# Attention scores from split operands: twelve-bit key and query halves on 128 rows, one full-array pass for each key tile, fetched per unit from DRAM

## The chip, the core and the metric

The kernel runs on one core of one Trainium2 chip. A core has five engines that run their own instruction streams and meet through semaphores: TensorE (PE, matrix products into PSUM; its weight loads have a row of their own in the profile, PEld), VectorE (DVE), ScalarE (ACT), GpSimd (POOL) and SyncE (SP, which here only issues DMA transfers). ACT and POOL can issue DMA transfers too. The metric is the device time of one execution in microseconds (us); lower is better.

## What is computed

Four images of 256 channels and 64 x 64 pixels go through a self-attention layer over the 4,096 pixels, and then through a clustering block with an MLP. The part that matters here is the attention's score matrix:

```python
C = 256
CQK = C // 8                       # 32
xf = x.reshape(B, Cc, N)           # N = 4096
q = jnp.einsum('oc,bcn->bno', wq, xf) + bq
k = jnp.einsum('oc,bcn->bon', wk, xf) + bk[None, :, None]
attn = jax.nn.softmax(jnp.einsum('bnd,bdm->bnm', q, k), axis=-1)
v = jnp.einsum('oc,bcn->bon', wv, xf) + bv[None, :, None]
out = jnp.einsum('bcn,bmn->bcm', v, attn).reshape(B, Cc, H, W)
x = gamma[0] * out + x
...
y = x + ls1 * cluster(group_norm(x))
y = y + ls2 * mlp(group_norm(y))
z = relu(batch_norm(y * dw_w)); z = relu(batch_norm(conv1x1(z, pw_w)))
```

A score is a product over only 32 values of the head, while every other large product is over 128 channels at a time. All inputs and outputs are float32.

## The kernel before

**Units.** The score matrix of an image is made transposed, keys on the 128 partitions and queries along the free axis. A *unit* is 512 keys (four tiles of 128) against one block of 512 queries; there are 8 x 8 = 64 units in an image, numbered u = 8 * nb + g with nb the query block and g the key group. `score(u)` (line 364) makes the four 128 x 512 tiles of a unit, copies them from PSUM to SBUF on ACT (lines 382 and 387) and takes the running maximum on DVE (lines 386 and 389). `exps(u)` subtracts the maximum (DVE, line 465), takes the exponential (ACT, line 468) and adds up the sums (POOL, line 473). `weigh(u, ...)` multiplies with the values (TensorE, line 478: eight matmuls a unit, "av" in the profile).

**Operands of the scores.** `k_half(i)` projects half of the keys (line 292) so that the key tile r of a group lies on partitions 32r to 32r + 31, and ACT evacuates it into the SBUF tile `k` (line 299). `q_four(i)` projects four query blocks, one on each 32 partitions (line 334), and ACT evacuates them (line 342). `q_block(nb)` (line 349) copies one block to all four groups of 32 partitions with four DMA transfers from SBUF to SBUF, issued on ACT's queue (on POOL's at the start, on SP's between images). Thus the four matmuls of a unit each use 32 rows of the array, on different rows.

**Order.** The order on every engine is written by hand. For each image:

- *Alone* (first image only): k_half(0), q_four(0), two q_blocks, then the units 0 to 7 with a pair of value projections (`v_pair`, line 315) after each; k_half(1) stands before unit 3.
- *Weighting*: 64 units; in unit u stand `exps(u + 1)`, `score(u + 10)` and the eight av matmuls of u. Each query block also has two row transfers through DRAM (`everywhere`, lines 84 and 85, SP's queue) that spread the maximum and the sum. `q_four(1)` stands at the end of unit 17.
- *Cluster* and *MLP*: while these run, the projections of the next image (`v_half`, `k_half`, `q_four`) are put in as filler at hand-chosen places by `fill(n)`. k_half(0) and q_four(0) stand after `similar(1)` and before `affine(0)` (line 819) and `largest(0)`, a chain on DVE that TensorE's product at line 904 waits for; k_half(1) stands before the second normalization. Eight scores of the next image, units 0 to 7, stand in the cluster's end and the MLP.

**Buffers.** SBUF tiles come from pools by tag. The tag "acc" has one buffer and is shared by the exponentials' sums, the odd normalized blocks, `g` (line 972) and the odd hidden tiles of the MLP; "w2" and "q4" also have one buffer each, "q" has two. A new tile under a tag waits until all readers of the last one are done. PSUM tag "m" has two buffers.

Of the kernel before, what the change touches and what calls it, by code (L numbers as in the profile page):

```python
# [7 lines left out]

F32 = mybir.dt.float32
AF = mybir.ActivationFunctionType  # L10
ALU = mybir.AluOpType
AX = mybir.AxisListType

P = 128
B, C, H, W = 4, 256, 64, 64
N = H * W
KC = C // P
NB = 512
NBLK = N // NB
XT = 1024  # L20
D = 32
# [7 lines left out]
RG, GRP = 4, N // NB  # L29
# [16 lines left out]
def attention_then_cluster_block(  # L46
# [17 lines left out]
    nc = tc.nc  # L64
# [3 lines left out]
    big = ctx.enter_context(tc.tile_pool(name="big", bufs=1))  # L68
# [4 lines left out]
    work = ctx.enter_context(tc.tile_pool(name="work", bufs=2))  # L73
# [202 lines left out]
    def attention(b, xs):  # L276
# [2 lines left out]
        own = {}  # L279
        stats = small.tile([P, 2 * NBLK, 6], F32, tag="stats", name=f"st1_{b}")  # L280
        cells = small.tile([P, KC, NBLK, 4], F32, tag="cells", name=f"cells_{b}")
        qs, slots, mxs, accs, tops, rdens, ts = {}, {}, {}, {}, {}, {}, {}

        def k_half(i):

            if i == 0:
                own["k"] = big.tile([P, GRP, P], F32, tag="k", name=f"k_{b}")
            ps = ps_m.tile([P, 2, 2, P], F32, tag="m", name=f"kp_{b}_{i}")
            for t in range(2):
                for k in range(KC):  # L290
                    for r in range(RG):
                        nc.tensor.matmul(
                            ps[r * D : (r + 1) * D, t],
                            wqk_s[:, k, 1],
                            xs[2 * i + t][:, k].rearrange("p (g r n) -> p r g n", g=2, r=RG)[:, r],
                            start=(k == 0),
                            stop=(k == KC - 1),
                        )
            nc.scalar.activation(
                own["k"][:, 4 * i : 4 * i + 4, :].rearrange("p (t g) n -> p t g n", t=2),  # L300
                ps,
                AF.Identity,
                bias=bqk_s[:, 1:2],
            )

        vps = {}

# [18 lines left out]
            v_half(2 * i)  # L326
            v_half(2 * i + 1)

        def q_four(i):

            ps = ps_m.tile([P, NB], F32, tag="m", name=f"qp_{b}_{i}")
            for k in range(KC):
                for r in range(RG):
                    nc.tensor.matmul(  # L334
                        ps[r * D : (r + 1) * D],
                        wqk_s[:, k, 0],
                        block(xs, k, 4 * i + r),
                        start=(k == 0),
                        stop=(k == KC - 1),
                    )  # L340
            own["q"] = work.tile([P, NB], F32, tag="q4", bufs=1, name=f"q4_{b}_{i}")
            nc.scalar.activation(own["q"], ps, AF.Identity, bias=bqk_s[:, 0:1])

        def q_block(nb, dma=nc.scalar):

            qs[nb] = work.tile([P, NB], F32, tag="q", name=f"q_{b}_{nb}")
            r = nb % 4
            for g in range(RG):
                dma.dma_start(
                    out=qs[nb][g * D : (g + 1) * D], in_=own["q"][r * D : (r + 1) * D]  # L350
                )

        def score(u, hooks=None, later=None):

            nb, g = divmod(u, GRP)
            q_s, k_s = qs[nb], own["k"]
            pool, tag = (swap, "w1") if u % (SLOTS + 1) == SLOTS else (spool, "s")
            s = slots[u] = pool.tile([P, RG, NB], F32, tag=tag, name=f"s_{b}_{u}")
            halves = [
                ps_s.tile([P, 2, NB], F32, tag="s", name=f"sc_{b}_{u}_{h}") for h in range(2)  # L360
            ]
            for r in range(RG):
                rows = slice(r * D, (r + 1) * D)
                nc.tensor.matmul(  # L364
                    halves[r // 2][:, r % 2, :], k_s[rows, g, :], q_s[rows, :], start=True, stop=True
                )
            if g == 0:
                tops[nb] = work.tile([P, 2, NB], F32, tag="top", bufs=1, name=f"top_{b}_{nb}")
# [163 lines left out]
        def alone():  # L532

            k_half(0)
            q_four(0)
            q_block(0, nc.gpsimd)
            q_block(1, nc.gpsimd)
            for i in range(4):
                v_pair(i)
            for u in range(GRP):  # L540
                if u == RG - 1:
                    k_half(1)
                hooks, maxima = [], []
                score(u, hooks, maxima)
                for f in hooks + maxima:
                    f()
                v_pair(u + 4)
            fold(0)
            for i in range(GRP + 4, GRP + 6):
                v_pair(i)  # L550
            half["dg"] = across(0)
            v_pair(GRP + 6)
            spread(0, half["dg"])
            v_pair(GRP + 7)
            exps(0)
            score(GRP)
# [26 lines left out]
        def weighting(ahead, fill, early):  # L583
# [3 lines left out]
            for u in range(units):  # L587
# [48 lines left out]
                        xs[t][:, c], xs[t][:, c], AF.Identity, bias=gbv[:, c : c + 1]  # L636
                    )
                if u == 2 * GRP + 1:
                    q_four(1)
                if g == 3 and nb + 2 < NBLK:  # L640
                    q_block(nb + 2)
                if g == GRP - 1 and more:
# [39 lines left out]

        parts = Parts()
        parts.xs, parts.alone, parts.weighting = xs, alone, weighting
        parts.score, parts.fold, parts.q_block = score, fold, q_block
        parts.maximum, parts.first, parts.exps = maximum, first, exps
        parts.projections = [lambda i=i: v_half(i) for i in range(N // P)]
        parts.projections[26:26] = [lambda: k_half(1)]
# [6 lines left out]
    def cluster(b, ys, stats, cells, rest, fill, gelu, nxt, maxima):  # L695
# [338 lines left out]
            fill(6)  # L1034
            return stats2

        nxt.q_block(0, nc.sync)
        fill(4)
        copies = []
        nxt.score(0, copies, maxima)  # L1040
# [120 lines left out]
    def mlp(b, ys, stats2, fill, nxt, blocks, turned, maxima):  # L1161
# [310 lines left out]
        for nb in range(blocks):  # L1472
            end = nb == blocks - 1
            for j in range(4):
# [12 lines left out]
                if j == 0:  # L1487
# [11 lines left out]
                    elif nxt:  # L1499

                        nc.sync.dma_start(
                            out=a21_s, in_=w2.rearrange("(k p) m -> p k m", p=P)[:, :h_n, P:]
                        )
                        nxt.q_block(1, nc.sync)
                elif j == 1:
                    assert not drips and not hooks
                    if nb:
# [155 lines left out]
```

## Time and profile before

| | before |
|---|---|
| median of 3 runs | 3339.82 us (3339.4 to 3340.23) |
| span of the profiled execution | 3338.8 us |
| mean granted TensorE clock | 0.997 of full speed |
| 256 units' scores: records on TensorE, busy time | 2,048, 299.8 us |
| av: records, busy time | 4,096, 1819.2 us |
| DMA traffic | 70.97 MB, 21 GB/s on average |

In the profile, "busy" of a group is the time in which at least one of its instructions ran; "mean" is one instruction from its start to its end, which is longer than the distance to the next, since matmuls overlap. "32*128" behind a matmul says how many rows and columns of the array it uses, "128x512" is partitions by elements, "idle before" is what the engine waited, and for whom. The chain of waits follows the last instruction back to whatever released it.

What the transfers cost, by the list of DMA issues (KB of each, and us from issue to landing):

```profile
out<-xn SPq DMA_DIRECT2D x62, 256.0 KB, 2.1
...
mr<-row_mx SPq DMA_DIRECT2D x28, 256.0 KB, 3.1
...
q<-q ACTq DMA_DIRECT2D x96, 64.0 KB, 2.0
```

And by the instructions of one line (lengths in ns, min/median/max, of the issue itself on its queue):

```profile
L349 ACTq DMA_DIRECT2D q<-q x96: 513/602/640, 92.7 to 2873.3; - x96
L349 SPq DMA_DIRECT2D q<-q x24: 513/582/1099, 617.8 to 2477.7; - x24
```
```profile
L1250 SPq DMA_DIRECT2D out<-xn x62: 332/332/1299, 694.5 to 3335.5; - x62
```

### The profile page before, as it was taken

Reading aid. Unit: us, or ns where it says so; the run is one execution under the profiler, and the core shown is the slowest. Engines: PE = TensorE matmul, PEld = TensorE weight load, DVE = VectorE, ACT = ScalarE, POOL = GpSimd, SP = SyncE. Lnnn points to the kernel's source line nnn. Section 1 sums busy time; section 2 is a strip of 40 time slices with the busy share of each in tenths; the row PEclk is TensorE's granted clock in tenths of the full one; section 3 lists DMA queues with packets and bytes.
Section 4 is the critical chain, followed back from the end, with each engine's and each line's share of the span. In section 5 each row is a group of like instructions: output and inputs, shape, how many; then the busy total and the mean of one; then the engine's idle time right before and its main releaser. Section 6 shows DMA issues by size and latency. Waiting matters only on the chain.

```text
span 3338.8 us, 34679 instructions
## 1 busy us (share of the span) xinstructions
PE 3299.9 (99%) x12266; PEld 1805.8 (54%) x12266; DVE 2221.8 (67%) x3554; ACT 1681.3 (50%) x2253; POOL 1929.7 (58%) x1366
## 2 busy tenths in 40 slices
PE   8999999999999999999999999999999999999999
PEld 4433444788533344578844334457873343446786
DVE  5667764677666766467766676647766766765675
ACT  5545553545555554355455555434556554544444
POOL 2655666366465675646646566554645666573664
PEclk9999999999999999999999999999999999999999
DMA  2000002000000000200000000010000000010000
GB/s 72 13 13 10 13 10 87 4 13 20 26 12 13 13 13 13 81 4 20 19 24 13 10 13 13 23 71 4 20 26 13 13 13 13 10 40 1 13 20 26
DMA packets 43101, 70.97 MB, mean 21 GB/s; under 512 B 9680, under 2 KB 18480, under 8 KB 42928
## 3 DMA queue, kind: packets, MB, share of 16 engines
q1 hardware_dynamic: 37040, 60.83, 5.5%
q10 hardware_dynamic: 5632, 7.41, 0.9%
q8 instruction: 96, 1.57, 0.2%
q0 software_dynamic: 256, 0.52, 0.1%
q14 instruction: 77, 0.63, 0.1%
HBM read 43.46 MB, written 16.89 MB: 18 GB/s over the span
## 4 chain that ended last, share of the span: by engine, by line
PE 94%; DVE 4%; ACT 1%; POOL 1%; issue 0%; DMA 0%; ACTq 0%; DVEq 0%; POOLq 0%
PE av L478 54%; PE mo L1294 9%; PE sc L364 8%; PE hq L1377 5%; PE hp L1377 3%; PE hr L1377 3%; PE fv L874 3%; PE vp L315 2%; PE mo L1278 1%; PE hq_pw L1377 1%; DVE st L979 1%; PE pw L1233 1%; PE hr_pw L1377 1%; PE hp_pw L1377 1%; DVE x L998 0%; PE qp L334 0%
## 5 line engine op out<-in xcount | busy, mean ns | idle before, releaser
L478 PE MATMUL av<-s,v 128*128 128x512 f32 x4096 | 1819.2, 598 | 0.6 <-ACT s L468 0.6
L473 POOL TENSOR_TENSOR acc<-acc,s 128x1024 f32<-128x1024 f32 x448 | 1057.0, 2359 | 539.1 <-ACT s L468 520.3
L478 PEld LDWEIGHTS av<-s,v 128*128 128x128 f32 x4096 | 759.1, 190 | 1044.7 <-issue 1034.7
L468 ACT ACTIVATE s<-s 128x1024 f32<-128x1024 f32 x512 | 540.1, 1057 | 591.1 <-DVE s L465 548.2
L465 DVE TENSOR_TENSOR s<-s,mb 128x1024 f32<-128x1024 f32 x512 | 595.8, 1206 | 18.1 <-ACT mb L449 16.4
L386 DVE TENSOR_TENSOR top<-sc,top 128x1024 f32<-128x1024 f32 x196 | 239.4, 1222 | 375.1 <-PE sc L364 375.0
L1332 ACT ACTIVATE hs<-hs,pv_s 128x256 f32<-128x256 f32 x496 | 232.2, 502 | 342.4 <-DVE hs L1368 342.4
L1294 PE MATMUL mo<-hs,w 128*128 128x256 f32 x1512 | 386.9, 382 | 0.0
L382 ACT COPY s<-sc 128x1024 f32<-128x1024 f32 x224 | 224.9, 1004 | 225.8 <-PE sc L364 225.8
L1294 PEld LDWEIGHTS mo<-hs,w 128*128 128x128 f32 x1512 | 282.6, 190 | 57.6 <-ACT hs L1332 19.6
L364 PE MATMUL sc<-q,k 32*128 32x512 f32 x2048 | 299.8, 640 | 0.5 <-ACT s L387 0.5
L389 DVE TENSOR_TENSOR top<-sc,top 128x1024 f32<-128x1024 f32 x196 | 240.1, 1225 | 71.8 <-ACT s L382 59.4
L387 ACT COPY s<-sc 128x1024 f32<-128x1024 f32 x224 | 227.1, 1014 | 66.4 <-DVE top L384 36.2
L1368 DVE TENSOR_TENSOR hs<-hq,hs 128x256 f32<-128x256 f32 x496 | 198.8, 421 | 78.2 <-PE hq L1377 67.9
L470 POOL TENSOR_TENSOR acc<-s 128x1024 f32<-128x1024 f32 x32 | 75.3, 2353 | 275.7 <-ACT s L468 275.7
L1301 POOL TENSOR_TENSOR hs<-hs 128x256 f32<-128x256 f32 x108 | 82.1, 761 | 190.9 <-ACT hs L1385 85.2
L364 PEld LDWEIGHTS sc<-q,k 32*128 32x128 f32 x2048 | 86.7, 182 | 183.1 <-issue 121.3
L1368 DVE TENSOR_TENSOR hs<-hp,hs 128x256 f32<-128x256 f32 x124 | 52.3, 421 | 125.8 <-ACT hs L1385 125.8
L315 PE MATMUL vp<-wv_s,x 128*128 128x256 f32 x512 | 127.8, 395 | 1.5 <-ACT v L323 1.5
L1377 PE MATMUL hr<-xn,w 128*128 128x256 f32 x496 | 128.1, 381 | 0.5 <-DVE hs L1368 0.5
L315 PEld LDWEIGHTS vp<-wv_s,x 128*128 128x128 f32 x512 | 95.4, 194 | 30.1 <-issue 12.7
L1377 PEld LDWEIGHTS hr<-xn,w 128*128 128x128 f32 x496 | 94.6, 191 | 18.1 <-issue 3.3
(262 smaller groups left out, 3491.2 us busy)
## 6 DMA issues: line engine op xcount, KB each, us to landing
out<-xn SPq DMA_DIRECT2D x62, 256.0 KB, 2.1
x<-in_x SPq DMA_DIRECT2D x30, 512.0 KB, 6.5
w<-in_w SPq DMA_DIRECT2D x8, 1024.0 KB, 10.2
mr<-row_mx SPq DMA_DIRECT2D x28, 256.0 KB, 3.1
rden<-row_rd SPq DMA_DIRECT2D x28, 256.0 KB, 3.1
q<-q ACTq DMA_DIRECT2D x96, 64.0 KB, 2.0
mix<-in_wfv SPq DMA_DIRECT2D x8, 192.0 KB, 7.8
q<-q SPq DMA_DIRECT2D x24, 64.0 KB, 2.0
```

What stands on the lines that cost most here:

```text
L315: nc.tensor.matmul(vps[0][:, i % 2, :], xs[i * P // XT][:, k, o : o + P], wv_s[:, k, :], start=(k == 0), stop=(k == KC - 1),)
L364: nc.tensor.matmul(halves[r // 2][:, r % 2, :], k_s[rows, g, :], q_s[rows, :], start=True, stop=True)
L386: nc.vector.tensor_tensor(top, halves[1], top, ALU.max)
L389: nc.vector.tensor_tensor(top, halves[0], top, ALU.max)
L465: nc.vector.tensor_tensor(sh, sh, mxs[nb].unsqueeze(1).to_broadcast([P, 2, NB]), ALU.subtract)
L468: nc.scalar.activation(sh, sh, AF.Exp)
L473: nc.gpsimd.tensor_tensor(acc, acc, s[:, 2 * h : 2 * h + 2], ALU.add)
L478: nc.tensor.matmul(av[c], own["v"][:, RG * g + quarter, c * P : (c + 1) * P], slots[u][:, quarter, :], start=(g == 0 and quarter == 0), st ...
L1294: return nc.tensor.matmul(bank[:, half * HB : (half + 1) * HB], a[:, j], t, start=start, stop=stop)
L1332: nc.scalar.activation(src, src, AF.Gelu_apprx_tanh, bias=pvc("b1", P, j + 4 * (i > 1)))
L1368: nc.vector.tensor_tensor(dst, ps, term, ALU.add)
L1377: nc.tensor.matmul(out, w, x, start=True, stop=True)
```

## The change

Keys and queries are split when they are evacuated from PSUM: ACT writes value + bias into a tile of type float32r (the high half, rounded to what that type holds), and DVE writes value + bias - high half (the low half), also as float32r. Both halves are written to a DRAM tensor of 128 rows, keys in the order high, low, high, low, queries in the order high, high, low, low, so that a product over the 128 rows is the sum of all four products of halves. `k_half` and `q_four` each issue 16 DMA writes on SP's queue for this; the first three of these evacuations in each image use the one buffer under "acc", `q_four(1)` uses "w2" and "q4".

`q_block` becomes one read of 256 KB from DRAM on SP's queue. A new function `k_unit(u)` reads the 128 x 512 keys of a unit (256 KB) into one of two buffers; `score(u)` asks for those of u + 1. Its four matmuls now use all 128 rows, with float32r operands. The order of everything else stays as it is.

```diff
@@ in attention()
+        def halves_of(ps, bias, tags, name):
+            if len(tags) == 1:
+                both = work.tile([P, 2, NB], F32R, tag=tags[0], bufs=1, name=f"hl_{name}")
+                hi, lo = both[:, 0], both[:, 1]
+            else:
+                hi, lo = (
+                    work.tile([P, NB], F32R, tag=t, bufs=1, name=f"hl{j}_{name}")
+                    for j, t in enumerate(tags)
+                )
+            nc.scalar.activation(hi, ps, AF.Identity, bias=bias)
+            nc.vector.scalar_tensor_tensor(
+                lo, ps, bias, hi.bitcast(F32), ALU.add, ALU.subtract
+            )
+            return hi, lo

         def k_half(i):
             if i == 0:
-                own["k"] = big.tile([P, GRP, P], F32, tag="k", name=f"k_{b}")
+                own["k"] = dram.tile([P, N], F32, tag="k", name=f"k_{b}")
+                own["q"] = dram.tile([P, N], F32, tag="q", name=f"q_{b}")
...
-            nc.scalar.activation(
-                own["k"][:, 4 * i : 4 * i + 4, :].rearrange("p (t g) n -> p t g n", t=2),
-                ps,
-                AF.Identity,
-                bias=bqk_s[:, 1:2],
-            )
+            parts = halves_of(ps, bqk_s[:, 1:2], ("acc",), f"k_{b}_{i}")
+            cols = own["k"][:, i * N // 2 : (i + 1) * N // 2]
+            for c in range(4):
+                rows = cols[c * D : (c + 1) * D].rearrange("d (g r n) -> d r g n", r=RG, n=P)
+                src = parts[c % 2].bitcast(F32).rearrange("p (g n) -> p g n", n=P)
+                for r in range(RG):
+                    nc.sync.dma_start(out=rows[:, r], in_=src[r * D : (r + 1) * D])

-        def q_four(i):
+        def q_four(i, tags=("acc",)):
...
-            own["q"] = work.tile([P, NB], F32, tag="q4", bufs=1, name=f"q4_{b}_{i}")
-            nc.scalar.activation(own["q"], ps, AF.Identity, bias=bqk_s[:, 0:1])
-
-        def q_block(nb, dma=nc.scalar):
-            qs[nb] = work.tile([P, NB], F32, tag="q", name=f"q_{b}_{nb}")
-            r = nb % 4
-            for g in range(RG):
-                dma.dma_start(
-                    out=qs[nb][g * D : (g + 1) * D], in_=own["q"][r * D : (r + 1) * D]
-                )
+            parts = halves_of(ps, bqk_s[:, 0:1], tags, f"q_{b}_{i}")
+            for c in range(4):
+                for r in range(RG):
+                    o = (4 * i + r) * NB
+                    nc.sync.dma_start(
+                        out=own["q"][c * D : (c + 1) * D, o : o + NB],
+                        in_=parts[c // 2][r * D : (r + 1) * D].bitcast(F32),
+                    )
+
+        def q_block(nb):
+            qs[nb] = work.tile([P, NB], F32R, tag="q", name=f"q_{b}_{nb}")
+            nc.sync.dma_start(out=qs[nb].bitcast(F32), in_=own["q"][:, nb * NB : (nb + 1) * NB])
+
+        def k_unit(u):
+            g = u % GRP
+            ks[u] = big.tile([P, NB], F32R, tag="k", bufs=2, name=f"k_{b}_{u}")
+            nc.sync.dma_start(out=ks[u].bitcast(F32), in_=own["k"][:, g * NB : (g + 1) * NB])

         def score(u, hooks=None, later=None):
             nb, g = divmod(u, GRP)
-            q_s, k_s = qs[nb], own["k"]
+            if u + 1 < units:
+                k_unit(u + 1)
+            q_s, k_s = qs[nb], ks.pop(u)
...
             for r in range(RG):
-                rows = slice(r * D, (r + 1) * D)
                 nc.tensor.matmul(
-                    halves[r // 2][:, r % 2, :], k_s[rows, g, :], q_s[rows, :], start=True, stop=True
+                    halves[r // 2][:, r % 2, :],
+                    k_s[:, r * P : (r + 1) * P],
+                    q_s,
+                    start=True,
+                    stop=True,
                 )
@@ in alone()
             k_half(0)
             q_four(0)
-            q_block(0, nc.gpsimd)
-            q_block(1, nc.gpsimd)
+            k_unit(0)
+            q_block(0)
+            q_block(1)
@@ in weighting()
                 if u == 2 * GRP + 1:
-                    q_four(1)
+                    q_four(1, ("w2", "q4"))
@@ in cluster() and mlp()
-        nxt.q_block(0, nc.sync)
+        nxt.q_block(0)
+        nxt.k_unit(0)
...
-                        nxt.q_block(1, nc.sync)
+                        nxt.q_block(1)
```

## The prediction

> **What bounds the kernel now.** I read the busy line and the chain of waits first, then the groups of TensorE instructions, and last the timeline around one score unit. Times are of the profiled execution: span 3338.8 us, 1.0 us under the median of the runs (3339.8 us).
>
> ```profile
> PE 3299.9 (99%) x12266; PEld 1805.8 (54%) x12266; DVE 2221.8 (67%) x3554; ACT 1681.3 (50%) x2253; POOL 1929.7 (58%) x1366
> ...
> PE av L478 54%; PE mo L1294 9%; PE sc L364 8%; PE hq L1377 5%; PE hp L1377 3%; PE hr L1377 3%; PE fv L874 3%; PE vp L315 2%; PE mo L1278 1%; PE hq_pw L1377 1%; DVE st L979 1%; PE pw L1233 1%; PE hr_pw L1377 1%; PE hp_pw L1377 1%; DVE x L998 0%; PE qp L334 0%
> ...
> L478 PE MATMUL av<-s,v 128*128 128x512 f32 x4096 | 1819.2, 598 | 0.6 <-ACT s L468 0.6
> ...
> L364 PE MATMUL sc<-q,k 32*128 32x512 f32 x2048 | 299.8, 640 | 0.5 <-ACT s L387 0.5
> ...
> L315 PE MATMUL vp<-wv_s,x 128*128 128x256 f32 x512 | 127.8, 395 | 1.5 <-ACT v L323 1.5
> ```
>
> TensorE is the bound and the scores (line 364) are on its path. The source has 1,024 score matmuls, the trace 2,048 records: each f32 matmul is two. Now the stretch in which unit follows unit:
>
> ```profile
> 299.95 1.14 PE L364 MATMUL sc<-q,k 32*128 32x512 f32 x8
> 301.02 7.13 PE L478 MATMUL av<-s,v 128*128 128x512 f32 x16
> 308.08 1.14 PE L364 MATMUL sc<-q,k 32*128 32x512 f32 x8
> 309.15 7.13 PE L478 MATMUL av<-s,v 128*128 128x512 f32 x16
> 316.22 1.14 PE L364 MATMUL sc<-q,k 32*128 32x512 f32 x8
> ```
> ```profile
> 299.94 0.31 PEld L364 LDWEIGHTS sc<-q,k 32*128 32x128 f32 x8 [0.76 <-issue]
> 301.01 0.30 PEld L478 LDWEIGHTS av<-s,v 128*128 128x128 f32 x2 [0.76 <-issue]
> ```
> ```profile
> 533.52 38.79 PE L478 MATMUL av<-s,v 128*128 128x512 f32 x90
> ```
>
> Columns are start, length, instruction, count. The period is 8.13 us. A run of av alone gives (38.79 - 0.60) / 89 = 0.429 us a record, so 16 take 6.86 and one unit's scores cost 8.13 - 6.86 = **1.27 us**. Streaming is only 2 x 0.429 = 0.86 of that, because the four row groups run side by side. The other 0.41 goes at the two changes of shape: weights, elsewhere loaded while the matmul before them runs, here start only once it has ended (0.76 us of idle in the weight loader instead of 0.24).
>
> **What the Trainium skill says.** "TensorEngine Tiling (Array Packing)", Key Properties: changing the tiling mode drains TensorE; the 0.41 us agrees. "FP8 and Floating Point Precision", TensorE Precision Notes: true FP32 takes four passes, high and low halves crossed, and a reduced-precision form reads the four bytes and truncates. Two records of 0.429 us for 512 columns fit four passes of 0.2145. "TensorE: Matmul & The Clock Gate", Back-to-back issue gap: one pass of N columns takes N/2.4 + 2.5 ns, 216 ns for 512; no float32r matmul is in this trace, but a record of line 315 streams as long (256 columns, two passes), and 32 of them in a row take 7.17 us, so (7.17 - 0.40) / 31 = 0.218 us each with their full 128-column weights hidden. The same page, HAM clock gate: after some 3.4 us of idleness the clock is halved and needs as long to return; the trace has 0.997 of full clock on average, so it has nearly none of this yet.
>
> **The change: what goes.** A unit's scores become four full-array matmuls of one pass, 4 x 0.2145 = 0.86 us. That is the old streaming time; the whole gain is the 0.41 us of the two mode changes. Do passes of another kind between f32 matmuls drain too? At 75.4 us two transposes stand amid av, and their weights are loaded ahead as usual:
>
> ```profile
> 74.96 0.19 PEld L478 LDWEIGHTS av<-s,v 128*128 128x128 f32 x1 [0.24 <-issue]
> 75.39 0.13 PEld L225 LDWEIGHTS wf_p<-ident,mix_first 128*96 128x96 f32 x1 [0.24 <-issue]
> ```
>
> So I take no drain; bounds 0 to 0.41 us back per unit. 223 units (55 of the first image, 56 of each other) are scored inside weighting and 24 in the MLP, where TensorE is as full: 247 x 0.41 = **101 us gained**. The period becomes 7.72 us; DVE (two subtractions at 1.21, two maxima at 1.22, about 1.2 of block work: 6.1) and POOL (two sums at 2.36 and block work: 5.5) stay under it.
>
> **What is added in steady state.** One 256 KB read per unit on SP's queue, asked for a unit ahead. The price lies between the 256 KB store (2.1 us to landing) and the 256 KB row broadcast (3.1); I take 0.33 to issue and 2.6 to land. It hides behind 7.7 us. SP serves in order: where a block's two row transfers stand ahead of it (row_mx at 243.18, mr at 244.53, scores wanting the key at 251.1) it lands near 247.5, and in the tightest place, behind rden, about 2 us of slack remain. In the MLP stage the reads stand behind output stores, but are wanted some 20 us later. q_block moves from ACT's queue (four issues at 0.60) to one on SP; that frees ACT, which isn't the bound.
>
> **What is added in bursts.** Every evacuation of k and q now costs ACT 0.69, DVE 0.75 (line 677's form) and 16 DRAM writes of 64 KB on SP. The price of issuing one lies between 0.33 (out<-xn, SBUF to DRAM) and 0.58 (q<-q on SP, 32 rows); I take 0.40, near the DRAM form: 6.4 us a burst, 2.0 to land. Four places are not hidden.
>
> (1) Start. SP is busy with constants until 19.67, and in the changed kernel's instruction order each transfer waits for the one eight before it, so k's eighth write goes at 24.3, when wpw_s lands (19.07 + 5.2), and its last lands near 29.9. q uses the same single buffer ("acc"), so ACT waits until then: 0.9 + 6.4 + 2.0, then the read 2.9: first score at 42 instead of 21.58, +20.5. At unit 4 the second k half is on the path: 0.7 + 6.4 + 2.0 + 2.9 = 12.0 us against 2.6 of TensorE work (a score, a v pair): +9.4. The eight-unit loop itself shortens by 0.3 a unit: -2.4. Sum **+27.5**.
>
> (2) q_four(1), unit 17 of each image. Unit 29's key read is queued behind 16 writes: 0.9 + 6.4 + 2.9 = 10.2 after qp ends, wanted after 7.7: 2.5 x 4 = **+10**.
>
> (3) The cluster stage of three images, where k_half(0) and q_four(0) are filler. Before:
>
> ```profile
> 615.57 0.29 DVE L819 TENSOR_SCALAR sg<-sg 128x256 f32<-128x256 f32 x1
> ...
> 616.52 0.67 ACT L299 ACTIVATE k<-kp,bqk_s 128x512 f32<-128x512 f32 x1
> 617.09 0.68 ACT L342 ACTIVATE q<-qp,bqk_s 128x512 f32<-128x512 f32 x1
> ...
> 621.53 1.53 PE L904 MATMUL agg<-vf,sim 128*32 128x96 f32 x64
> ```
>
> Now DVE's low half of q stands ahead of line 819, and it waits for ACT's high half, which waits until k's 16 writes have left "acc": 617.2 + 0.2 + 6.4 + 1.9, then 0.9 and 0.8 on the two engines: line 819 starts at 627.4, 11.8 late. Everything behind it on DVE, and so TensorE's agg at 621.5, moves with it; behind ACT's wait stand two v copies, so the filler stops too. k's low half before the second normalization adds 0.75. 3 x 12.55 = **+37.7**.
>
> (4) Five of these stalls (start two, cluster three) outlast 3.4 us; if each costs half of 3.4 us of clock, +8.5 (estimate from the clock-gate page; 0 to 8.5).
>
> **Sum:** 101.3 - 27.5 - 10 - 37.7 - 8.5 = 17.6 gained; 3338.8 - 17.6 + 1.0 = **3322 us**.
>
> **Rivals.**
>
> *B, the write bursts cost more.* Place: the ten bursts that end on the path (three at the start, four at unit 17, three in the cluster stage), 160 writes. Break-even is 0.40 + 17.6/160 = 0.51 us a write. At the 0.58 of q<-q, the only 32-row transfer on SP in the trace, +29: 3351, slower. For it: same rows, same queue. Against: that one writes SBUF; the two stores to DRAM (out 0.33, row_mx 0.32) are cheap.
>
> *C, the score still breaks the weight pull-ahead.* float32r is another form than the transposes, and each score's first matmul now waits on two semaphores (a DMA and ACT). Half the 0.41 kept: 3373; all of it: 3423.
>
> *D, float32r streams at half rate*, 0.429 a matmul because four bytes are read: +0.86 x 247 = 212, 3534. Against: the four-pass account above. Were the tiles run as plain f32 (the change not doing what it says), it would be worse still; 2,048 records would show it.
>
> **How the numbers follow.** A (as summed) 0.50, own range 3302 (0.33 a write and no clock loss) to 3340; B 0.22; C 0.18; D 0.10. About 0.2% (6.7 us) is what can be told from no change. A is faster 0.40, same 0.07, slower 0.03; B 0.01, 0.04, 0.17; C and D slower. Together faster 0.41, same 0.11, slower 0.48: the likeliest single case is a gain, but it rests on a difference of two sums near 100 us. The range 3300 to 3420 takes in A, B and nearly all of C and leaves D and some of each edge out, near 0.2.
>
> **What would show it.** Score records halve to 1,024 of 128*128; unit period 7.72 (8.13: C; 8.6: D). First score near 42 us. SP's k and q writes at 0.40 each. Line 819's successor some 12 us after its sg product, with ACT's wait for DMA ahead of it. A stall of 2 to 3 us one unit after each q_four(1). Wrong if TensorE waits for key reads in ordinary units, or if the period doesn't fall.

## The result, and the profile after

The changed kernel takes 3350.25 us (median of 7 runs, 3346.32 to 3354.39); the kernel before, beside it, 3339.99 (3339.4 to 3340.34). The ratio is 1.0032, 95% interval 1.0021 to 1.0043: slower by 10 us, where 18 us less had been forecast. The profiled execution has a span of 3352.4 us, 13.6 more than before, and a mean granted clock of 0.985 instead of 0.997.

The page of the changed kernel: first the busy line, then groups of instructions (records, busy time, mean ns of one; then the idle time before them and what ended it).

```profile
PE 3236.9 (97%) x11242; PEld 1943.3 (58%) x11242; DVE 2231.0 (67%) x3570; ACT 1678.8 (50%) x2253; POOL 1930.9 (58%) x1358
...
L337 PE MATMUL vp<-wv_s,x 128*128 128x256 f32 x512 | 137.7, 417 | 39.9 <-ACT v L345 39.3
...
L395 PE MATMUL sc<-q,k 128*128 128x512 f32 x1024 | 370.9, 484 | 30.9 <-DMA k<-k 24.6
```

The score records have halved to 1,024, so the new operands are used as meant, and TensorE is busy 63 us less. But it is no longer full: it stands 39.9 us before value projections (for ACT) and 30.9 us before scores (24.6 of it for transfers of keys), where before it stood 1.5 and 0.5. The units that follow each other without a stall, on TensorE and in the weight loader:

```profile
333.87 1.49 PE L395 MATMUL sc<-q,k 128*128 128x512 f32 x4
335.20 7.03 PE L513 MATMUL av<-s,v 128*128 128x512 f32 x16
341.66 1.49 PE L395 MATMUL sc<-q,k 128*128 128x512 f32 x4
```
```profile
334.27 0.65 PEld L395 LDWEIGHTS sc<-q,k 128*128 128x128 f32 x3 [0.24 <-issue]
334.97 0.42 PEld L513 LDWEIGHTS av<-s,v 128*128 128x128 f32 x2
```

The period is 341.66 - 333.87 = 7.79 us instead of 8.13, and weights are loaded ahead again (0.24 us of idle or none, where before it was 0.76 at each change of shape). Minus sixteen av records at 0.429, a unit's scores cost 0.93 us, not 0.86.

Now the places where TensorE stands. The start (TensorE and SP):

```profile
42.14 2.04 PE L395 MATMUL sc<-q,k 128*128 128x512 f32 x4 [4.34 <-DMA q<-q]
...
66.85 2.05 PE L395 MATMUL sc<-q,k 128*128 128x512 f32 x4 [10.37 <-DMA k<-k]
```
```profile
19.44 7.72 SPq L326 DMA_DIRECT2D k<-hl_k  x16
29.41 7.37 SPq L367 DMA_DIRECT2D q<-hl_q  x16
...
54.40 7.92 SPq L326 DMA_DIRECT2D k<-hl_k  x16
```

The first score comes at 42.14 us (before: 21.58), that of unit 4 waits 10.4 us for its keys. The score of unit 8 starts at 88.8 instead of 57.2: 31.6 us lost. Behind `q_four(1)` in image 1, TensorE and SP together:

```profile
1062.38 7.67 SPq L367 DMA_DIRECT2D q<-hl_q  x16
...
1073.35 2.05 PE L395 MATMUL sc<-q,k 128*128 128x512 f32 x4 [3.84 <-DMA k<-k]
```
```profile
1075.19 9.11 PE L513 MATMUL av<-s,v 128*128 128x512 f32 x16
```

The key read stands behind 16 writes, the score waits 3.84 us, and then sixteen av records take 9.11 us instead of 7.03: the granted clock is half of full speed from 1072.5 to 1079.4 us. In images 2 and 3 a wait of 3.4 and 3.5 us is followed by half the clock too; in image 0 one of 3.49 us is not. And the cluster stage of image 0, all engines:

```profile
635.25 8.66 SPq L326 DMA_DIRECT2D k<-hl_k  x16
...
645.45 0.69 ACT L298 ACTIVATE hl_q<-qp,bqk_s 128x512 fp32r<-128x512 f32 x1 [10.22 <-DMA k<-hl_k]
...
646.66 3.78 PE L337 MATMUL vp<-wv_s,x 128*128 128x256 f32 x8 [8.61 <-ACT v L345]
646.84 0.28 DVE L855 TENSOR_SCALAR sg<-sg 128x256 f32<-128x256 f32 x1
...
652.37 3.02 PE L940 MATMUL agg<-vf,sim 128*32 128x96 f32 x64 [1.93 <-DVE sim L870]
```

ACT's high half of q waits 10.2 us for the key writes to leave "acc". Behind it wait the low half and the gathering on DVE (L855, 819 before) and the value projections on TensorE; the product `agg` comes 62.1 us after the stage's first product instead of 49.3, 12.8 us later, and takes 3.02 us instead of 1.53.

The sum over the span:

| | forecast, us | measured, us |
|---|---|---|
| scores in weighting and MLP | -101.3 | -83.8 |
| start, to the score of unit 8 | +27.5, clock +3.4 | +31.6 |
| around unit 17, four images | +10 | +22.2 |
| three cluster stages | +37.7, clock +5.1 | +43.6 |
| sum | -17.6 | +13.6 |

The start and the cluster stages are differences between the same instructions in the two traces. Around unit 17 that difference is +18.1; the row has 4.1 more, because the gain of the twelve units there (0.345 us each) is counted in the first row. The first row is the rest of the span's difference; a direct count over 233 units gives -80.0 us, 0.343 each, which with those 4.1 agrees. A stage of the clusters runs here from the division's first product (`den`) over `agg` to the second normalization's mean.

### The profile page after: what moved, and what is told of

Its sections match the earlier page's. It is cut to its first block, busy times and chain, and to the rows that moved or that the text cites. A ratio compares the mean times of both kernels' runs of the same rounds, so it can differ in the third digit from the quotient of the medians.

```text
span 3352.4 us, 33609 instructions
## 1 busy us (share of the span) xinstructions
PE 3236.9 (97%) x11242; PEld 1943.3 (58%) x11242; DVE 2231.0 (67%) x3570; ACT 1678.8 (50%) x2253; POOL 1930.9 (58%) x1358
## 3 DMA queue, kind: packets, MB, share of 16 engines
q10 hardware_dynamic: 1024, 1.12, 0.1%
## 4 chain that ended last, share of the span: by engine, by line
PE 89%; DVE 4%; SPq 2%; ACT 1%; DMA 1%; issue 1%; POOL 1%; ACTq 0%; DVEq 0%; POOLq 0%
PE av L513 50%; PE mo L1331 9%; PE sc L395 7%; PE hq L1414 5%; PE hp L1414 3%; PE hr L1414 3%; PE fv L910 3%; PE vp L337 2%; PE mo L1315 1%; SPq L326 1%; SPq L367 1%; PE hq_pw L1414 1%; PE pw L1270 1%; PE hr_pw L1414 1%; PE hp_pw L1414 1%
## 5 line engine op out<-in xcount | busy, mean ns | idle before, releaser
L513 PE MATMUL av<-s,v 128*128 128x512 f32 x4096 | 1800.1, 593 | 0.7 <-ACT s L503 0.7
L513 PEld LDWEIGHTS av<-s,v 128*128 128x128 f32 x4096 | 778.3, 190 | 898.4 <-issue 868.8
L395 PE MATMUL sc<-q,k 128*128 128x512 f32 x1024 | 370.9, 484 | 30.9 <-DMA k<-k 24.6
L395 PEld LDWEIGHTS sc<-q,k 128*128 128x128 f32 x1024 | 191.1, 191 | 174.4 <-issue 127.4
L337 PE MATMUL vp<-wv_s,x 128*128 128x256 f32 x512 | 137.7, 417 | 39.9 <-ACT v L345 39.3
L337 PEld LDWEIGHTS vp<-wv_s,x 128*128 128x128 f32 x512 | 102.3, 207 | 67.5 <-ACT v L345 43.2
L1047 POOL TENSOR_TENSOR x<-cl,x 128x512 f32<-128x512 f32 x32 | 40.0, 1278 | 120.6 <-ACT cl L1046 120.6
```

The lines of the kernel that those rows point to most:

```text
L337: nc.tensor.matmul(vps[0][:, i % 2, :], xs[i * P // XT][:, k, o : o + P], wv_s[:, k, :], start=(k == 0), stop=(k == KC - 1),)
L395: nc.tensor.matmul(halves[r // 2][:, r % 2, :], k_s[:, r * P : (r + 1) * P], q_s, start=True, stop=True,)
L513: nc.tensor.matmul(av[c], own["v"][:, RG * g + quarter, c * P : (c + 1) * P], slots[u][:, quarter, :], start=(g == 0 and quarter == 0), st ...
```

## The experiments

Two questions: what the bursts of writes cost and through what, and why a score unit gained 0.345 us and not 0.41. The table has the three kinds of places for every kernel that moved one of them; agg to mean is the rest of the cluster stage. Rows that begin with "and" add their edit to the kernel with few writes and two buffers; the last two of these also have POOL's queue.

| kernel | median, us | score of unit 8 at | den to agg, three images | agg to mean |
|---|---|---|---|---|
| before | 3340 | 57.2 | 49.3, 49.3, 49.3 | 21.6, 21.6, 21.6 |
| changed | 3350.25 | 88.8 | 62.1, 61.2, 62.3 | 23.8, 23.5, 23.4 |
| two buffers | 3322.0 | 85.7 | 51.9, 51.9, 51.9 | 23.7, 23.8, 22.4 |
| read first | 3331.55 | 85.7 | 61.9, 61.2, 61.3 | 24.1, 23.1, 22.4 |
| few writes | 3299.3 | 70.1 | 54.8, 56.8, 54.8 | 24.2, 23.7, 23.8 |
| few writes, two buffers | 3288.85 | 67.3 | 51.9, 51.9, 51.9 | 23.8, 23.5, 22.4 |
| and POOL's queue | 3284.79 | 66.0 | 51.8, 51.9, 51.9 | 23.8, 23.8, 22.4 |
| and chain first | 3291.3 | 63.9 | 56.0, 56.5, 55.8 | 22.1, 22.1, 22.1 |
| chain first, alone | 3351.81 | 88.0 | 61.9, 62.0, 62.6 | 23.0, 23.4, 22.7 |
| and half the chain first | 3274.72 | 65.2 | 50.3, 50.3, 50.3 | 22.3, 22.3, 22.3 |

### Two buffers for the first query halves

```diff
-            q_four(0)
+            q_four(0, ("w2", "q4"))
...
-        parts.projections[16:16] = [lambda: k_half(0), lambda: q_four(0)]
+        parts.projections[16:16] = [lambda: k_half(0), lambda: q_four(0, ("w2", "q4"))]
```

> The changed kernel with one thing altered: the query halves of q_four(0) get two buffers of their own (the tags w2 and q4, as q_four(1) has them), so that they do not wait for the key halves' 16 writes out of acc. My theory (the 43.6 us that the three cluster stages lost are ACT and DVE standing at that one buffer): den to agg sim falls from 62 us to 50 to 52 and the start loses 2 us (the query writes follow the key writes without the gap from 27.2 to 29.4), so about 40 us less than the changed kernel, 3310 us. Rival (the stage is late because SP's queue is full of writes, or because of the extra DVE and ACT operations themselves): the ACT wait on key writes goes, but the stage stays near 62 us and the kernel near 3350.

Measured: 3322.0 us, ratio to before 0.9943 (0.9928 to 0.9958). One buffer tag turns the loss into a gain. The wait on "acc" was the main cause in the cluster stages: den to agg loses 30 us over the three. But 2.6 us a stage stay up to `agg` and, in two of the three images, some 2 us behind it, and 28 us came back in all where 40 were expected. What these are was open until the reorderings below.

### The key read ahead of the writes

```diff
@@ score()
-            if u + 1 < units:
+            if u + 1 < units and u + 1 not in ks:
                 k_unit(u + 1)
@@ weighting()
                 if u == 2 * GRP + 1:
+                    k_unit(u + LEAD + 2)
                     q_four(1, ("w2", "q4"))
```

> The changed kernel with the key read of unit 29 issued ahead of q_four(1)'s 16 writes instead of behind them on SP. My theory (the 22.2 us lost around unit 17 are a score that waits for a key read queued behind 7.7 us of issues, about 3.9 us an image, and the halved clock after it): the wait of 3.8 us before that score goes, the loss falls to 0.5 to 1 us an image, and the kernel takes about 18 us less, 3332 us. Rival (the wait comes from the read's landing among the writes' traffic, or the loss comes from q_four's projection work and evacuation): the wait only moves to the next unit or stays, under 5 us gained, 3346 to 3352.

Measured: 3331.55 us, ratio 0.9975 (0.9964 to 0.9986), 18.7 below the changed kernel, as expected. The score that had waited 3.84 us in image 1, and the av behind it:

```profile
1062.28 1.48 PE L395 MATMUL sc<-q,k 128*128 128x512 f32 x4
1063.60 7.03 PE L513 MATMUL av<-s,v 128*128 128x512 f32 x16
```

No score around there waits, and the clock stays full. The unit with `qp` takes 10.14 us where 9.99 - 0.345 was due, and the next is 0.3 us shorter than usual, so that 0.2 us an image are left of the 22.2. The order of one read against 16 writes in SP's queue was the whole stall, and the halved clock its consequence.

### Few writes

The halves are written to DRAM as they lie on the chip, two writes of 128 rows for each evacuation, and the reads gather them, four of 32 rows for one of 128. `q_four` and `q_block` are changed in the same way as the two functions shown.

```diff
-                own["k"] = dram.tile([P, N], F32, tag="k", name=f"k_{b}")
+                own["k"] = dram.tile([4 * P, NB], F32, tag="k", name=f"k_{b}")
@@ k_half()
-            for c in range(4):
...
-                for r in range(RG):
-                    nc.sync.dma_start(out=rows[:, r], in_=src[r * D : (r + 1) * D])
+            for h in range(2):
+                o = (2 * i + h) * P
+                nc.sync.dma_start(out=own["k"][o : o + P], in_=parts[h].bitcast(F32))
@@ k_unit()
-            nc.sync.dma_start(out=ks[u].bitcast(F32), in_=own["k"][:, g * NB : (g + 1) * NB])
+            for c in range(4):
+                o = (2 * (g // 4) + c % 2) * P
+                src = own["k"][o : o + P].rearrange("(r d) (g n) -> d r g n", r=RG, n=P)
+                nc.sync.dma_start(
+                    out=ks[u][c * D : (c + 1) * D].bitcast(F32).rearrange("p (r n) -> p r n", n=P),
+                    in_=src[:, :, g % 4],
+                )
```

> The changed kernel with keys and queries kept in DRAM as they lie on chip, [512 rows, 512]: 2 writes of 128 rows for each evacuation instead of 16 of 32 rows, and 4 reads of 32 rows for each key tile and query block instead of one of 128. My theory (the number of writes is what costs: 16 issues at 0.43 to 0.45 us each): at the start 2 x 14 x 0.44 = 12 us and the 10.4 us stall of unit 4 go, the buffer wait in each cluster stage falls from 14 to about 2 or 3 us (35 to 40 us in all), the stall after q_four(1) goes (18 us): 3350 - 70 = 3280 us, with 3265 to 3300. Rival (the bytes and landings of the writes cost, not their number): the key writes still hold acc for 8 us or more and the kernel stays above 3325. A second rival: four reads of 32 rows with 512-byte runs land too late for a period of 7.8 us, and every unit waits for its keys (the period rises above 8).

And the same with the two query buffers:

> The few writes and the two query buffers together. My theory: the second has little left to free when the key halves leave acc after 2 writes, so 3 to 8 us below the kernel with few writes alone, about 3275 us. Rival (the one buffer costs something apart from the number of writes, such as the DVE operation that stands ahead of the gathering): 15 us or more below it.

Measured: 3299.3 us (ratio 0.988, 0.9865 to 0.9894) and 3288.85 us (0.9846, 0.983 to 0.9863). The number of writes costs, not their bytes. The issues of the few-writes kernel (KB each, us from issue to landing):

```profile
k<-k SPq DMA_DIRECT2D x1024, 64.0 KB, 2.1
...
k<-hl_k SPq DMA_DIRECT2D x16, 256.0 KB, 2.0
```

In the changed kernel a write of 64 KB lands after 1.8 us and a whole key read after 3.0. The Trainium skill's "DMA: Bandwidth & Descriptors", Anatomy of one DMA, has that nearly all of a small transfer is a fixed part of some 2 us (stated for transfers issued by POOL; the writes on SP's queue agree: four times the bytes, 0.2 us more). So the bytes hardly matter to the landing. The length of a burst is made by its issues: 16 of them, 0.43 us each in the median, fill SP's queue for over 7 us, two for 1.1. Four reads a unit instead of one leave the period at 7.79 us. In 11 units behind the start a score waits 0.1 to 0.65 us, mostly for its keys, 3.7 us in all (0.3 in the changed kernel, the waits behind `q_four(1)` apart), which may be their price. The start wins 18.7 us and the stalls behind `q_four(1)` go. The cluster stage, though, won only 19 us up to `agg` where 35 to 40 over the whole stage were expected: the single buffer still makes ACT wait 3 us there, and the same 2 to 3 us as in the two-buffer kernel stay. With both, the stage stands where two buffers alone had put it, and the second edit is worth 10 us, between its two expectations.

### What a score pass costs

Three kernels measure it; one leaves out the key reads to see whether their traffic has a part in it.

```diff
@@ scores twice: changed kernel, score()
-            for r in range(RG):
+            for r in (0, 1, 2, 3, 0, 1, 2, 3):
@@ half columns: changed kernel, score()
-            for r in range(RG):
+            for r, o in [(r, o) for r in range(RG) for o in (0, NB // 2)]:
...
-                    halves[r // 2][:, r % 2, :],
+                    halves[r // 2][:, r % 2, o : o + NB // 2],
...
-                    q_s,
+                    q_s[:, o : o + NB // 2],
@@ twice before: kernel before, score()
-            for r in range(RG):
+            for r in (0, 1, 2, 3, 0, 1, 2, 3):
@@ no key reads: changed kernel, k_unit()
-            ks[u] = big.tile([P, NB], F32R, tag="k", bufs=2, name=f"k_{b}_{u}")
+            if u:
+                ks[u] = own["kt"]
+                return
+            own["kt"] = ks[u] = big.tile([P, NB], F32R, tag="k", bufs=2, name=f"k_{b}_{u}")
```

> The changed kernel with the four full-array score passes of each unit issued twice into the same tiles (same values). It measures the price of four such passes by themselves. My theory (one pass of 512 columns of this type costs 0.2325 us wherever it stands, 0.0180 more than the 0.2145 that two records of true float32 add up to): a period of 7.79 + 0.93 = 8.72 us and 256 x 0.93 = 238 us more than the changed kernel. Rival (a pass is 0.2145 us and the 0.07 us a unit that my sum missed belong to the change-over between the scores and the weighting): a period of 8.65 us and 220 us more.

> The changed kernel with each score pass of 512 columns made as two of 256 columns with the same weights (same values, twice the weight loads). If a pass is bound by its columns: period 7.79, no change. My theory (the columns plus a small constant a pass, 0.2325 = 0.2145 + 0.0180): 4 x 0.018 = 0.07 us a unit more, a period of 7.86, 18 us in all. Rival (a pass is bound by the load of its 128x128 weights, the next load taking 0.23 us): eight passes at 0.23 make a period of 8.72 and 235 us more.

> The kernel before with the four row-tiled score matmuls of each unit issued twice into the same tiles (same values). It splits the 1.27 us that a unit's scores cost there. As my prediction has it (0.86 us of streaming and 0.41 us at the two changes of tiling, which a second set does not repeat): period 8.13 + 0.86 = 8.99, 256 x 0.86 = 220 us more than the kernel before. Rival (nothing is lost at the changes; row-tiled passes of true float32 cost 0.32 us each): period 9.40, 325 us more. Second rival (nearly the whole price is the change of tiling, and the four row tiles stream side by side): under 0.5 us a unit, 125 us or less.

> The changed kernel without the key reads but the first of each image: every unit scores against key tile 0 (the scores of the other key tiles are left out), so 63 of 64 reads of 256 KB are gone. My theory (in ordinary units the reads are hidden behind a whole period): the period stays 7.79 us; what goes is the stall of unit 4 (10.4 us) and the stalls after q_four(1) (18 us), so 3322 us; the cluster stages stay at 62 us. Rival (the traffic of the reads slows the passes by 0.07 us a unit, my missing 17 us): the period falls to 7.72 and the time to 3305.

TensorE with the scores issued twice, first in the changed kernel and then in the kernel before:

```profile
211.20 2.39 PE L395 MATMUL sc<-q,k 128*128 128x512 f32 x8
213.43 7.03 PE L513 MATMUL av<-s,v 128*128 128x512 f32 x16
219.89 2.39 PE L395 MATMUL sc<-q,k 128*128 128x512 f32 x8
```
```profile
305.83 2.00 PE L364 MATMUL sc<-q,k 32*128 32x512 f32 x16
307.76 7.13 PE L478 MATMUL av<-s,v 128*128 128x512 f32 x16
314.82 2.00 PE L364 MATMUL sc<-q,k 32*128 32x512 f32 x16
```

In the kernel before, a second set makes the period 314.82 - 305.83 = 8.99 us, 0.86 more; time 3555.98 us. This is the prediction's figure: 0.86 us of streaming, and the other 0.41 belong to the changes of tiling, since a second set doesn't pay them again.

In the changed kernel a second set makes it 219.89 - 211.20 = 8.69, 0.90 more: 0.225 us a pass, between the two expectations of 0.2325 and 0.2145, of which neither came true. The time, 3567.35 us or 217 more, fits the lower one, but it is the weaker witness, because some stalls of the changed kernel shrink when units are longer (the unit before the score that waits behind `q_four(1)` is 2.9 us over its period here in image 0, against 3.8). So of the 0.93 us, 0.90 are the four passes and 0.03 the change-over. TensorE with half columns:

```profile
336.18 1.51 PE L395 MATMUL sc<-q,k 128*128 128x256 f32 x8
337.54 7.03 PE L513 MATMUL av<-s,v 128*128 128x512 f32 x16
344.00 1.51 PE L395 MATMUL sc<-q,k 128*128 128x256 f32 x8
```

The period is 7.82 us (3361.05 us): eight weight loads and eight passes cost 0.03 us more than four, so the passes are bound by their columns and not by their weights, and the constant of 0.018 us a pass that had been expected isn't there. Without key reads the period stays 7.79: their traffic costs TensorE nothing. That kernel takes 3315.55 us, 35 less than the changed one, because both places where a score waits for keys are gone (the score of unit 8 starts at 72.7 us, 16 earlier; the 22 us around unit 17); 28 had been expected.

### POOL's queue at the start

From the kernel with few writes and two buffers (`k_half`, `q_four` and `q_block` take the issuing queue as an argument):

```diff
-            k_half(0)
-            q_four(0, ("w2", "q4"))
+            k_half(0, nc.gpsimd)
+            q_four(0, ("w2", "q4"), nc.gpsimd)
             k_unit(0)
-            q_block(0)
-            q_block(1)
+            q_block(0, nc.gpsimd)
+            q_block(1, nc.gpsimd)
...
-                if u == RG - 1:
+                if u == 1:
                     k_half(1)
```

> Few writes, two query buffers, and the start of the program rearranged: the first image's key and query writes and its first two query blocks go by POOL's queue, which is idle there, instead of standing behind six constants on SP, and k_half(1) comes after unit 0 instead of after unit 2. My theory (with few writes, the start is bound by the key write that issues on SP at 18.8 us though its halves are ready at 14.6): the first score comes 4 us earlier, at about 24 us, unit 4's stall of 3.8 us goes, and the kernel takes 3289 - 7 = 3282 us. Rival (POOL issues DMAs more slowly, 0.52 us each in the kernel before, and has the constants' products to make at 21.5 us, or the landings take over): no gain, 3287 to 3292.

Measured: 3284.79 us, ratio 0.9833 (0.9819 to 0.9846), an interval that overlaps that of the kernel it started from: nothing can be claimed. The first score comes at 26.7 us, not 24, and the stall moved from unit 4 to unit 2 (2.7 us for its keys). The Trainium skill's "DMA: Bandwidth & Descriptors", Issuing engines are not separate DMA queues, has that another issuing engine saves sequencer time only, and here this was little: the score of unit 8 starts 1.3 us earlier.

### The order of DVE's work in the cluster stage

The kernel with POOL's queue, with the chain `affine` to `weights` put ahead of k_half(0) and q_four(0), and the same edit alone on the changed kernel:

```diff
         similar(1)
+        affine(0)
+        largest(0)
+        affine(1)
+        largest(1)
+        weights(0)
+        weights(1)
         fill(2)
         summed(lambda j, q: pool_w[:, j], True)
         gelu(1)
         fill(4)
         table(AF.Sqrt)
-        affine(0)
...
-        weights(1)
```

> The kernel with few writes, two query buffers and POOL's queue at the start, and one thing more: the DVE chain of the gathering (affine to weights, lines 858 to 873 of its code) is issued ahead of k_half(0) and q_four(0), so the two low-half subtractions stand behind it instead of ahead of it. My theory (the 2.56 us that den to agg sim still has over the kernel before, 51.86 against 49.30, are that DVE chain waiting for the evacuations, and the 2 us after it the halved clock that follows TensorE's idle time): den to agg sim falls to 49.3, agg sim to the second norm's mean falls from 23.5 to about 22, and the kernel takes 3285 - 12 = 3273 us. Rival (the rest of the stage's loss comes from the work itself, ACT or TensorE being busy longer): within 3 us of 3285.

> The changed kernel with only that reordering of the DVE chain: 16 writes and the single buffer stay. It tells through which engine the single buffer delays the stage. If through DVE (the low half of q stands ahead of the gathering, as my prediction had it), the chain is free of it now and the three stages fall from 62 to about 50 us: 3350 - 37 = 3313. If through ACT and the PSUM buffers (the copies of v wait behind the query's high half on ACT, and TensorE's next value projections wait for a free tile ahead of the agg matmuls), the stages stay within 2 us of 62 and the kernel at 3344 to 3352.

Measured: 3291.3 us (0.9856, 0.9839 to 0.9872) and 3351.81 us (1.0039, 1.0024 to 1.0054). The first is a miss, with the sign wrong: den to agg grew by 4 us. The second tells why. Its cluster stage in image 0, all engines:

```profile
639.73 0.75 DVE L870 TENSOR_TENSOR sim<-sg,scr 128x256 f32<-128x256 f32 x2
...
641.19 3.51 PE L337 MATMUL vp<-wv_s,x 128*128 128x256 f32 x8 [4.06 <-DVE hl_k L299]
...
649.58 3.78 PE L337 MATMUL vp<-wv_s,x 128*128 128x256 f32 x8 [4.88 <-ACT v L345]
```

The chain is done at 640.5 us, 12 earlier than in the changed kernel, and `agg` still starts at 653.3. In TensorE's order four value projections stand ahead of `agg`, and they need PSUM tiles: the first one needs the tile of k's projection, which the low half of k frees (moved behind the chain, hence 4.06 us), a later one a tile whose copy waits on ACT behind the high half of q. So the single buffer delays the stage by two ways, DVE's chain and these projections. In the changed kernel they end 2 us apart (`agg` waits for the chain 1.93 us after the last projection), so that taking away DVE's way could gain about 2 us. It gained nothing, because this order also lengthens the other way: the key writes wait for their low half and take 10.45 us instead of 8.66, and ACT's high half of q waits 12.0 us instead of 10.2. Hence a third reordering, again from the kernel with POOL's queue, which moves only the first half of the chain:

```diff
         similar(1)
+        affine(0)
+        largest(0)
         fill(2)
...
-        affine(0)
-        largest(0)
         affine(1)
```

> As the kernel with POOL's queue at the start, with only the first half of the gathering's DVE chain (affine(0), largest(0)) ahead of k_half(0) and q_four(0). The first half needs 2.5 us from where the low halves used to wait, and they are fed at 1.97 us, so the low half of k is late by under 1 us and the rest of the chain early by 1 us. My theory (both ends of the stage hang on DVE's order: the value projections wait for the tile that the low half of k frees, and the agg matmuls for the chain): den to agg sim falls from 51.86 to about 50.9, TensorE's idle time there from 2.3 to under 1.5 us, and with it goes the halved clock of the agg matmuls (3.02 to 1.53 us): 2.5 to 4 us an image, 3285 - 10 = 3275 us. Rival (the tile of k is the nearer limit, as in the reordering of the whole chain, which lost 4 us an image): den to agg sim stays or grows, 3284 to 3290.

Measured: 3274.72 us (3273.38 to 3277.0), ratio 0.9807 (0.9794 to 0.982), at the expected value; its slowest run is 5 us faster than the fastest of the kernel with POOL's queue. Its stage, all engines:

```profile
610.66 3.72 PE L334 MATMUL vp<-wv_s,x 128*128 128x256 f32 x16 [0.91 <-DVE hl_k L299]
...
614.31 1.68 PE L943 MATMUL agg<-vf,sim 128*32 128x96 f32 x64
```

The projections wait 0.9 us, `agg` follows them without idle time (2.34 us in the kernel with POOL's queue) and runs at 1.68 us instead of 3.02; den to agg is 50.3 and the rest of the stage 22.3, nearly as before the change. This version is 65 us faster than the kernel before and 75 faster than the changed one; mean granted clock 0.996.

## Why the prediction was wrong

**The gain, 101 us.** Half of its working held. The split of 1.27 us into 0.86 of streaming and 0.41 of mode changes is shown by the doubled scores of the kernel before (+0.86); weights are loaded ahead again, so rival C is out, and no pass is at half rate, so D is out. The term that failed is "four full-array matmuls of one pass, 4 x 0.2145 = 0.86". A pass of this form costs 0.225 us, and entering and leaving them 0.03: 0.93. So a unit gained 0.345 us, and the whole term -83.8: **17.5 us short**, of which the passes are some 10 (247 x 4 x 0.0105) and the change-over, taken as nothing with bounds of 0 to 0.41, some 7 (247 x 0.03). The figure of 0.2145 had been taken from records of another form, half of a true float32 matmul, and 0.01 us a pass was enough to matter a thousand times. The 0.218 us of the line 315 records, also in the prediction, would have been nearer but not right.

**Unit 17, 10 us.** The mechanism (unit 29's read behind 16 writes) is shown by the reordered read. The size was wrong: 22.2 us. The four stalls were 3.4 to 3.8 us each and not 2.5 (in image 1 the 16 writes took 7.67 us instead of 6.4 and the read some 3.2 us instead of 2.9) and make some 15 us. The halved clock was not counted at all here (the prediction gave that to five other stalls): the unit behind the stall takes 10.4, 9.1 and 9.1 us in images 1 to 3 and 7.5 in image 0, where the clock stayed full, so some 6 us. The last 0.8 are there without a stall too. **12.2 us short.** These two terms are 29.7 of the 31.2 us between forecast and trace.

**Start, 27.5 us and clock.** Held: +31.6 against 30.9; first score at 42.14 against 42; unit 4 stalled 10.4 against 9.4. That the first score comes so close is in part luck. The last key write landed at 28.5 us and not at 29.9 (the transfer that it was to wait for landed at 21.8 us, not 24.3), and the query read was issued at 37.3, before the last query write landed at 38.2, where the sum has it wait; both made up for a burst of 7.4 us instead of 6.4 and for a read that took 4.7 us instead of 2.9.

**Cluster stage, 37.7 us and clock.** Held in size: 43.6 against 42.8. As to the way, the prediction named DVE as the path, and `agg` does wait for DVE last. The way over the value copies on ACT, which it named only as a filler that stops, ends just 2 us earlier, and the order that frees DVE's chain lengthens it: with DVE's part gone, the stage is as long as before.

**The price of a write, rival B.** The ten bursts on the path took 7.37 to 8.70 us, 0.49 us a write on average, against 0.40 in the sum and 0.51 at break-even. So B's direction was right, by its own sum for 14 of the 17.6 us, and it explains part of unit 17; but in the start and the cluster stage the sums held all the same, and what put the kernel on the other side was the score pass and unit 17 with its clock. That the 3350 us lie on B's 3351 is chance: B has 0.58 us a write. The forecast of a gain was a difference of two sums near 100 us, as it said; errors of 17% in the gain (83.8 us against 101.3) and 16% in the loss (97.4 against 83.7 with the clock), both to the worse side, were enough.

## What to carry to other kernels

When data goes on a detour through DRAM, count the transfers, not the bytes: here 16 writes of 64 KB held their queue, their source buffer and everything behind both for about 10 us, 2 of 256 KB for about 3, and a latency-bound read that is due belongs ahead of them in the queue. Give two evacuations that follow each other two buffers; a single one couples engines that had nothing to do with each other. And where a stage waits by two ways that end within a few us of each other, removing one moves little or nothing: look at every in-order queue that ends at the late instruction.

## What the runs showed of the hardware that was not expected

A float32r pass of 512 columns over the full array costs 0.225 us at the margin, 0.0105 more than half of a true float32 matmul of the same shape (0.429 / 2), though both stream 512 columns. Where the rest goes is open: splitting a pass in two added only 0.0075 us, so at most that much is a constant of the pass.

The clock: the Trainium skill's "TensorE: Matmul & The Clock Gate", Part 1: The HAM clock gate, has a free-running window of about 3.4 us of activity. The traces agree as to the window: in all fourteen, the changes of the granted clock lie multiples of 3.413 us apart. But a stall need not be as long as the window. Before `agg`, images 0 and 2 of the kernel with POOL's queue:

```profile
616.50 3.02 PE L943 MATMUL agg<-vf,sim 128*32 128x96 f32 x64 [2.34 <-DVE sim L873]
...
2241.66 1.76 PE L943 MATMUL agg<-vf,sim 128*32 128x96 f32 x64 [2.34 <-DVE sim L873]
```

The idle time is the same. In image 0 it lies within one window (613.1 to 616.5 us), and the next window has half the clock; in image 2 the edge of a window splits it into 1.94 and 0.40 us, and the clock stays full. In the same way the stall of 3.49 us in image 0 of the changed kernel, longer than a window but split into 1.74 and 1.75 us, cost no clock, and that of 3.84 us in image 1, 3.03 of it in one window, did. Counted over the fourteen traces: of the windows at full clock in which TensorE stood for more than 2.05 us, all 116 were followed by one at half clock, and of those in which it stood for less than 1.3 us, none. In between both occur (the profile models the ends of matmuls, so these times are rough). So a stall shorter than the window can cost more than its own length: the order that took those 2.34 us away also took 1.3 us off `agg` and 1.5 off what follows in two of three images.
